# Where the first feed-forward gets its transposed input: in its own blocks, or from layer 0's attention by way of memory

## The chip, the core and the metric

The kernel runs on one core of a Trainium2 chip, in one launch. The metric is the device time of the launch in microseconds (us). A core has five engines that run side by side, each through its own queue of instructions: TensorE (PE in the profile: matrix products and transposes), VectorE (DVE), ScalarE (ACT), GpSimd (POOL) and SyncE (SP, which here only issues transfers). Transfers between the memory outside and the on-chip memory run on 16 DMA engines; SP's queue and POOL's queue both issue them.

## The reference, cut to what matters

Two gated blocks over x, 4 x 1024 rows of 512 numbers. In each, the row is normalised, attention gives s, a feed-forward gives a gate, and x becomes x + s * silu(gate):

```python
x = L0_attn_x
xn = _layernorm(x, axis=-1)                       # eps 1e-5
s = _L0_attn_ref(xn, Wqkv, bqkv, Wout, bout, slopes)
g = _silu(_L0_ffn_ref(xn, w_fc, w_proj))
x = x + s * g
# ... the same again with layer 1's attention and feed-forward

def bitlinear(x, w):                              # in _L0_ffn_ref, twice
    xn = layer_norm(x)                            # eps 1e-6
    ...
    return jnp.einsum('bsd,od->bso', x_hat, w_hat)
```

Layer 0's attention is linear attention with decay, in chunks with a running state. Its input and the feed-forward's input are the same rows: the first bitlinear normalises the already normalised row once more. Doing that a second time only multiplies the row by one number per row (per token), 1 / sqrt(variance of the normalised row + 1e-6).

## The kernel before, in words

The 4096 rows are cut into 8 blocks of 512 (`BLK`), a block into 4 tiles of 128 rows (`TPB`). A block's transposed rows are held as four slabs of 128 features x 512 tokens (`KD`). The program has four stages, one after the other: attention of layer 0, the feed-forward of layer 0, attention of layer 1, the feed-forward of layer 1. The change touches the first two.

**Attention of layer 0** (L234 to L544) is a loop of 32 steps (L506): block `blk`, head group `g` from 0 to 3. A step's products on TensorE are, in this order: `scores` of this step; `project`, which makes queries and keys of the next step from `xnTs[blk]`; a first job (`output` of the block before for g < 2, `values` of the block after for g >= 2); `outs`; the transposes of keys (`turn_k`); for g < 2 two tiles of the next block's rows normalised and transposed (`turn0`); the second job; the product for the state (`states`). Around them, ScalarE adds the bias to kT and qT (L355) and copies `oT` (L451); VectorE weighs the scores into `pt` (L422), makes `kd` (L374), adds the bias to values (L328) and to outputs (L338), and keeps the state; GpSimd makes `qd` (L357). Beside that, two jobs a step from `weights0` load a 256 KB piece of the feed-forward's weights each (`raw0`, two buffers) and reduce it or turn it into its ternary form on VectorE.

`moments0` takes mean and variance of the next block's rows in step g = 0; `norms0` (L302) makes the second normalisation's factor from them and multiplies it with the first one's (L308), so that `st[:, :, 3]` is one factor for both. The normalised rows `xn` have a tag of two buffers; the slabs `xnT` have two as well, so block `blk + 2` overwrites block `blk`; the tag `s` for outputs has two. The single-bank accumulators in PSUM (`acc`) also rotate over two: an accumulator can be started when the one two before it has been read out.

**The feed-forward's input.** Its products take the input as two parts, `hi` (the number rounded to the matmul's format, fp32r) and `lo` (the rest), each 128 x 4 x 512, from `xpair` (tags xp0 and xp1, two buffers each). In attention all four of these buffers hold `wqkv` and a few constants (L255). For block 0 the parts are made in the last step by `first_rows` (L453): x is loaded again (L542), VectorE makes `xq` with the one factor, TensorE transposes it, and `split_in` (L227) copies hi on ScalarE and subtracts lo on VectorE. For the other blocks this is done in the feed-forward itself.

**The feed-forward of layer 0** (L552 to L743) runs over 8 blocks x 16 hidden chunks c. `hidden` multiplies the chunk (8 matmuls, L594), ScalarE applies gelu, casts and squares, VectorE subtracts the low part `hp` (L607), and the sums of h and of its square are kept on GpSimd (L615) and VectorE (L616). `proj` (L647, 8 matmuls a chunk) follows two to eight chunks behind. In blocks 0 to 6, x of the next block is loaded at c = 0, 3, 6 and 9 (L714), `prep_in` makes xq at c = 2, 5, 8 and 11 (L574), and one chunk later `turn_in` transposes it on TensorE (L582) and splits it. `gate` of the block before (L652) comes at c = 1, 3, 5 and 7; it loads x and s. In block 0, six weight pieces are still loaded and made ternary (L718).

**Order.** TensorE's order is written by hand: within `manual_schedule` it runs its instructions as the program lists them. The order on the other queues, SP's included, is chosen when the kernel is built, by when each operation is expected to be ready, and is fixed from then on: an instruction that waits holds up all behind it. `keep_in_program_order` pins an instruction behind the one that the program lists just before it on the same queue; it doesn't hold back later ones that are not pinned. The pools with `reuse_waits="tile"` make the first writer of a buffer wait only for the readers of the tile that had it before.

Of the kernel before, what the change touches and what calls it, by code (L numbers as in the profile page):

```python
# [35 lines left out]
def kernel(ctx, tc, ins, out):  # L36
# [59 lines left out]
    nc.vector.memset(one_i, 1)  # L96

    xnT_d = [dram.tile([KD, P, N], F32, tag=f"xnT{b}", name=f"xnT_d{b}") for b in range(B)]

    def moments(pool, src, dst, name, pinned=False):  # L100

# [122 lines left out]
            w = nxt  # L224
            yield

    def split_in(xp, i, tp):  # L227

        hi, lo = [a[:, :, i * P : (i + 1) * P] for a in xp]
        nc.scalar.copy(hi.bitcast(F32R), tp)  # L230
        nc.vector.tensor_tensor(lo.bitcast(F32R), tp, hi, ALU.subtract)


    with ExitStack() as es:  # L234
# [52 lines left out]


        xnTs, vs, oTs = {}, {}, {}
        xparts = {}  # L290

        def moments0(blk):
            st = st0[blk]
            for i in range(TPB):
# [7 lines left out]
        def norms0(blk):  # L302

            st = st0[blk]
            nc.vector.tensor_tensor(st[:, :, 3], st[:, :, 1], st[:, :, 1], ALU.mult)
            nc.vector.tensor_tensor(st[:, :, 3], st[:, :, 3], st[:, :, 2], ALU.mult)
            inv_std(st[:, :, 3], eps6)
            nc.vector.tensor_tensor(st[:, :, 3], st[:, :, 3], st[:, :, 1], ALU.mult)  # L308

        def turn0(blk, i):  # L310
            st = st0[blk]
# [138 lines left out]
            oTs[blk, g] = p2.tile([P, BLK], F32, tag="oT", name=f"oT0_{nm}", bufs=6)  # L450
            nc.scalar.copy(oTs[blk, g], o)  # L451

        def first_rows(i0):  # L453

            st = st0[0]
            for i in range(i0, i0 + 2):
                xq = p2.tile([P, D], F32, tag="xn", name=f"xq_{i}")
                nc.vector.tensor_scalar(
                    xq, xt.pop(i), st[:, i, 0:1], st[:, i, 3:4], ALU.subtract, ALU.mult
                )  # L460
                tp = tr(f"tr_xq_{i}")
                for k in range(KD):
                    nc.tensor.transpose(tp[:, k, :], xq[:, k * P : (k + 1) * P], ident)
                split_in(xparts[0], i, tp)

        es.enter_context(tc.manual_schedule(engines={mybir.EngineType.PE}))

        st = st0[0]
# [37 lines left out]
        for n, (blk, g) in enumerate(steps):  # L506

            if g < 2:
                jobs = [(output, blk - 1, 2 * g + c) for c in range(2)] if blk else []
            else:  # L510
                jobs = [(values, blk + 1, 2 * g - 4 + c) for c in range(2)] if blk + 1 < NBLK else []
            if n + 1 == len(steps):
                xparts[0] = xpair("xp_0")
                jobs = [(first_rows, 0), (first_rows, 2)]
            if g == 0 and blk + 1 < NBLK:
                moments0(blk + 1)
            pts = scores(blk, g, *cur[:2])
# [34 lines left out]
    with ExitStack() as es:  # L552
# [5 lines left out]
        def tr0(name):  # L558
            return pp.tile([P, KD, P], F32, tag="tr", name=name)

        hparts, sums, mvs, x1s, xnTp, x0fs = {}, {}, {}, {}, {}, {}
# [4 lines left out]
        def prep_in(blk, i):  # L566

            st = st0[blk]
            if i == 0:
                xparts[blk] = xpair(f"xp_{blk}")  # L570
            t = blk * TPB + i
            x = x0fs.pop(t)
            xq = p2.tile([P, D], F32, tag="xq", name=f"xq_{t}")
            nc.vector.tensor_scalar(  # L574
                xq, x, st[:, i, 0:1], st[:, i, 3:4], ALU.subtract, ALU.mult
            )
            return lambda: turn_in(blk, i, xq)

        def turn_in(blk, i, xq):
            tp = tr0(f"tr_xq_{blk}_{i}")  # L580
            for k in range(KD):
                nc.tensor.transpose(tp[:, k, :], xq[:, k * P : (k + 1) * P], ident)  # L582
            split_in(xparts[blk], i, tp)

        before = None

# [65 lines left out]
        def gate(blk, i):  # L652

            t = blk * TPB + i
            mv = mvs[blk]

            last = blk == NBLK - 1 and i >= 2
            x = p2.tile([P, D], F32, tag="x" if last else "xr", name=f"x0r_{t}")
            nc.sync.dma_start(out=x, in_=x_t[t])
            s = p2.tile([P, D], F32, tag="xq" if last else "s", name=f"s0_{t}")  # L660
# [12 lines left out]
            queue.dma_start(out=x1_t[t], in_=th)  # L673
            moments(p2, th, st1[:, t, :], f"c{t}")
# [19 lines left out]
                )  # L694

        es.enter_context(tc.manual_schedule(engines={mybir.EngineType.PE}))
        pending = None
        W = {}
        for g in range(NH0 * NBLK + 2 + 2 * TPB):
            blk, c = divmod(g, NH0)  # L700
            if g == NH0 * NBLK:

                for n in ("wk", "wq", "wv"):
                    W[n] = shared_tile(n, n)
                    tc.keep_in_program_order(
                        nc.gpsimd.dma_start(
                            out=W[n], in_=ins[n + "T"].rearrange("(k p) n -> p k n", p=P)
                        )
                    )
            if blk < NBLK:  # L710
                if c % 3 == 0 and c < 3 * TPB and blk + 1 < NBLK:
                    t = (blk + 1) * TPB + c // 3
                    x0fs[t] = p2.tile([P, D], F32, tag="x", name=f"x0f_{t}")
                    nc.sync.dma_start(out=x0fs[t], in_=x_t[t])  # L714
                if c >= 2 and c % 3 == 2 and c < 2 + 3 * TPB and blk + 1 < NBLK:
                    pending = prep_in(blk + 1, (c - 2) // 3)
                hidden(blk, c)
                if blk == 0 and wpj0 + c < NH0:  # L718
                    ternary("pj", wpj0 + c, raw0("pj", wpj0 + c, "f"))
            for i in range(TPB):  # L720
                q = g - 2 - 2 * i
                if 0 <= q < NH0 * NBLK:
                    proj(q // NH0, i, q % NH0)
            if c == 0 and blk == 1:
                rps = tr0("rows_ps").rearrange("p k c -> p (k c)")
                for w in range(NH0):
                    nc.tensor.matmul(
                        rps, lhsT=onesr, rhs=wpj[w], start=(w == 0), stop=(w == NH0 - 1)
                    )
                nc.scalar.copy(rows, rps)  # L730
            if blk and c == 1:
                stats(blk - 1)
            if blk and c % 2 and c < 2 * TPB:
                gate(blk - 1, c // 2)
            if blk and c == 12:
                norm1(blk - 1, p2)
            if pending and c % 3 == 0:
                pending()
                pending = None
# [764 lines left out]
```

## Time and profile before

| what | value |
|---|---|
| median of 3 runs | 3135.22 us (3134.12 to 3144.06) |
| the profiled execution | 3134.57 us, its span 3132.7 us, mean granted TensorE clock 0.996 |
| attention of layer 0 | 0 to about 605 us, then its last outputs to 620 us |
| feed-forward of layer 0 | 620 to about 1154 us |
| HBM traffic | 104.10 MB read, 41.94 MB written, 47 GB/s over the span |

A row of the profile's groups names a line of the kernel, the engine, the operation, output <- input by the program's names with buffer numbers left out, the shapes, how often it ran, and min/median/max in nanoseconds or busy microseconds and the mean. A row of the timeline begins with start and length in us; in brackets at its end stands the idle time of that engine before it, and what ended it. A row of busy times by stretch gives the stretch and its length, then for each engine its busy us and the number of its records, then the granted clock (1.00 is full speed), the DMA engines' busy share and GB/s. PE is TensorE's matmuls, PEld its weight loads, SPq and POOLq the issue of transfers. Matmuls are pipelined, so the sum of their lengths is more than the time they take.

### The profile page before, as it was taken

The numbers are of one execution on the slowest core, as the hardware profiler recorded it, in microseconds if no ns is written. First come the engines' busy times: TensorE is split into PE (matmuls) and PEld (weight loads), VectorE is DVE, ScalarE is ACT, GpSimd is POOL, SyncE is SP. The second block draws the span as 40 slices with busy tenths as digits, with TensorE's granted clock in tenths as the row PEclk, the third lists the DMA queues.
The fourth block names the chain that finished last, engine by engine and source line by source line (L and its number), as shares of the span: only waits on it lengthen the run. The fifth ranks groups of instructions, "written<-read, shape, count | busy, mean of one in ns | idle before, by whom it ended". The sixth has DMA issues, their size and how long they took to land.

```text
span 3132.7 us, 61075 instructions
## 1 busy us (share of the span) xinstructions
PE 3074.4 (98%) x26241; PEld 1757.1 (56%) x26241; DVE 1878.7 (60%) x2620; ACT 1195.2 (38%) x1696; POOL 1476.2 (47%) x614
## 2 busy tenths in 40 slices
PE   9999999999999997999999999999999999999998
PEld 5555555577777873443344443334444435888887
DVE  4444555478887775556655555555555674566655
ACT  3111111155556542444444444444444444333332
POOL 0000000034443443898888988888888850000001
PEclk9999999999999998999999999999999999999999
DMA  3111111112222331100001000010000013322211
GB/s 132 55 54 61 54 55 41 58 55 87 85 75 68 108 126 39 47 8 8 7 17 41 12 12 15 17 38 13 10 17 12 12 48 112 108 78 64 68 51 55
DMA packets 97543, 158.46 MB, mean 51 GB/s; under 512 B 13040, under 2 KB 26864, under 8 KB 97136
## 3 DMA queue, kind: packets, MB, share of 16 engines
q1 hardware_dynamic: 96128, 150.28, 15.5%
q8 instruction: 207, 3.39, 0.5%
q0 software_dynamic: 1136, 4.19, 0.4%
q14 instruction: 72, 0.59, 0.1%
HBM read 104.10 MB, written 41.94 MB: 47 GB/s over the span
## 4 chain that ended last, share of the span: by engine, by line
PE 58%; DVE 1%; ACT 1%; issue 0%; SPq 0%; DMA 0%; ACTq 0%; DVEq 0%
PE sk L1033 9%; PE sq L1006 8%; PE y L1052 8%; PE gate L1236 5%; PE up L1236 5%; PE dn L1258 5%; PE wq L862 4%; PE v1ps L862 3%; PE wo L862 3%; PE wk L862 3%; PE sk L1039 2%; PE z L946 1%; ACT pT L1044 1%; DVE mT L1022 1%; PE tr_m L1016 1%; DVE mx L1010 0%
## 5 line engine op out<-in xcount | busy, mean ns | idle before, releaser
L1010 DVE TENSOR_REDUCE mx<-sq 128x2 f32<-128x1024 f32 x512 | 603.4, 1218 | 392.5 <-PE sq L1006 391.2
L1075 POOL TENSOR_TENSOR part<-part,pT 128x2048 f32<-128x2048 f32 x180 | 826.7, 4593 | 19.6 <-ACT pT L1044 10.8
L1044 ACT ACTIVATE pT<-sk 128x1024 f32<-128x1024 f32 x512 | 496.2, 1021 | 611.9 <-PE sk L1039 606.8
L1006 PE MATMUL sq<-wkT,wqT 32*128 32x512 f32 x2048 | 321.3, 640 | 13.3 <-POOL wqT L920 7.2
L1033 PE MATMUL sk<-wqT,wkT 32*128 32x512 f32 x2048 | 326.0, 639 | 4.1 <-DVE mx L1010 3.8
L1052 PE MATMUL y<-pT,v 128*32 128x512 f32 x2048 | 273.7, 605 | 0.1
L615 POOL TENSOR_TENSOR sums<-sums,h 128x512 f32<-128x512 f32 x112 | 164.0, 1465 | 227.6 <-ACT h L599 222.4
L647 PE MATMUL pj<-wpj,hp 128*128 128x512 f32 x1024 | 265.2, 397 | 5.8 <-DVE hp L607 4.8
L594 PE MATMUL fc<-xp,wfc 128*128 128x512 f32 x1024 | 260.8, 397 | 2.9 <-ACT h L599 2.0
L1280 POOL TENSOR_TENSOR th<-th,x 128x512 f32<-128x512 f32 x31 | 40.1, 1295 | 457.6 <-DVE th L1279 378.9
L1039 PE MATMUL sk<-mT,onesr 2*128 2x512 f32 x1024 | 236.6, 785 | 0.0
L350 PE MATMUL qk<-xnT,wqkv 128*128 128x512 f32 x512 | 228.3, 599 | 0.7 <-ACT xnT L148 0.7
L357 POOL TENSOR_TENSOR qd<-qT,wqkv 128x512 f32<-128x512 f32 x32 | 40.7, 1272 | 397.3 <-ACT qT L355 372.2
L647 PEld LDWEIGHTS pj<-wpj,hp 128*128 128x128 f32 x1024 | 189.9, 188 | 58.0 <-DVE hp L607 17.4
L594 PEld LDWEIGHTS fc<-xp,wfc 128*128 128x128 f32 x1024 | 187.3, 188 | 44.3 <-ACT h L599 5.1
L1236 PE MATMUL gate<-xp,wf 128*128 128x512 f32 x704 | 174.1, 389 | 0.0
L1236 PE MATMUL up<-xp,wf 128*128 128x512 f32 x704 | 173.9, 389 | 0.0
L1258 PE MATMUL dn<-wf,hp 128*128 128x512 f32 x704 | 173.6, 389 | 0.0
L1033 PEld LDWEIGHTS sk<-wqT,wkT 32*128 32x128 f32 x2048 | 98.0, 183 | 133.5 <-issue 109.8
L1073 POOL TENSOR_TENSOR part<-pT,pT 128x2048 f32<-128x2048 f32 x30 | 136.7, 4558 | 67.6 <-ACT pT L1044 67.4
L607 DVE TENSOR_TENSOR hp<-h,hp 128x512 fp32r<-128x512 f32 x128 | 117.1, 915 | 76.2 <-ACT hp L604 76.2
L1006 PEld LDWEIGHTS sq<-wkT,wqT 32*128 32x128 f32 x2048 | 89.5, 183 | 125.9 <-issue 83.4
(229 smaller groups left out, 4512.4 us busy)
## 6 DMA issues: line engine op xcount, KB each, us to landing
s<-s SPq DMA_DIRECT2D x96, 256.0 KB
x<-x SPq DMA_DIRECT2D x36, 256.0 KB
x<-in_x SPq DMA_DIRECT2D x32, 256.0 KB
raw_fc<-in_w_fcT SPq DMA_DIRECT2D x32, 256.0 KB
x0f<-in_x SPq DMA_DIRECT2D x32, 256.0 KB
x0r<-in_x SPq DMA_DIRECT2D x32, 256.0 KB
xnT<-xnT_d SPq DMA_DIRECT2D x8, 1024.0 KB
s<-so SPq DMA_DIRECT2D x32, 256.0 KB
```

What stands on the lines that cost most here:

```text
L594: nc.tensor.matmul(a, lhsT=wfc[k][:, c * P : (c + 1) * P], rhs=xp[n][:, k, :].bitcast(F32R), start=(k == 0 and n == 0), stop=(k == KD - 1 ...
L647: nc.tensor.matmul(ds[i], lhsT=hparts[blk, c][n][:, i * P : (i + 1) * P], rhs=wpj[c], start=(c == 0 and n == 0), stop=(c == NH0 - 1 and n ...
L862: nc.tensor.matmul(out[r0 : r0 + HD, :], lhsT=lhsT[:, r0 : r0 + HD], rhs=rhs, start=start, stop=stop,)
L1006: nc.tensor.matmul(sq[:, hh, :], lhsT=qT[r, q0 : q0 + P], rhs=kT[r, n * 512 : (n + 1) * 512], start=True, stop=True,)
L1010: nc.vector.tensor_reduce(mx[:, qt, 2 * pair : 2 * pair + 2, n], sq, AX.X, ALU.max)
L1033: nc.tensor.matmul(sks[h // 2][:, h % 2, :], lhsT=kT[r, kb * P : (kb + 1) * P], rhs=qT[r, qh * 512 : (qh + 1) * 512], start=True, stop=False,)
L1039: nc.tensor.matmul(sks[h // 2][:, h % 2, :], lhsT=onesr[r, :], rhs=mTs[u][r, :], start=False, stop=True,)
L1044: nc.scalar.activation(pT[:, 2 * pair : 2 * pair + 2, :], sks[pair], AF.Exp, scale=QKS)
L1052: nc.tensor.matmul(y[r, :], lhsT=v[:, kb, r], rhs=pT[:, h, :], start=(kb == 0), stop=(kb == TB - 1),)
L1075: add.tensor_tensor(parts[u], parts[u], pT, ALU.add)
L1236: nc.tensor.matmul(a, lhsT=ws[n, c][:, k, :], rhs=xp[m][:, k, :], start=(k == 0 and m == 0), stop=(k == KD - 1 and m == 1),)
L1258: nc.tensor.matmul(ds[i], lhsT=hparts[blk, c][n][:, i * P : (i + 1) * P], rhs=w, start=(c == 0 and n == 0), stop=(c == NH1 - 1 and n == 1),)
```

## The change

The 1e-6 factor is no longer multiplied into the 1e-5 one; its 512 numbers for a block are stored in memory by POOL's queue. At the end of step g = 2 of each block, `scale` loads them back as one row on all partitions and GpSimd multiplies the block's four slabs with it in place: after that step no product of attention reads the slabs any more. In step g = 3, before `outs`, `split` makes hi on ScalarE (in the two buffers of the tag xn) and lo on VectorE (in place), slab by slab, and POOL's queue stores both in memory: eight transfers of 256 KB a block, 16.8 MB in all. `ffn_in` loads a block's two parts, 1 MB each, on SP's queue: for block 0 at the end of the last step but one of attention, for the others at c = 1 of the block before. `first_rows`, `prep_in`, `turn_in`, `split_in`, their reloads of x and their 128 transposes are gone.

```diff
+    xp0_d = [
+        [dram.tile([KD, P, BLK], F32, tag=f"xp0_{i}_{m}", name=f"xp0_d{i}_{m}") for m in range(2)]
+        for i in range(NBLK)
+    ]
+    more_d = dram.tile([NBLK, BLK], F32, tag="more", name="more_d")
...
-    def split_in(xp, i, tp):
-
-        hi, lo = [a[:, :, i * P : (i + 1) * P] for a in xp]
-        nc.scalar.copy(hi.bitcast(F32R), tp)
-        nc.vector.tensor_tensor(lo.bitcast(F32R), tp, hi, ALU.subtract)
+    def ffn_in(blk):
+
+        xparts[blk] = xpair(f"xp_{blk}")
+        for m in range(2):
+            tc.keep_in_program_order(
+                nc.sync.dma_start(out=xparts[blk][m], in_=xp0_d[blk][m].rearrange("k p n -> p k n"))
+            )
...
             inv_std(st[:, :, 3], eps6)
-            nc.vector.tensor_tensor(st[:, :, 3], st[:, :, 3], st[:, :, 1], ALU.mult)
+            nc.gpsimd.dma_start(out=more_d[blk].rearrange("(i p) -> p i", p=P), in_=st[:, :, 3])
+
+        def scale(blk):
+
+            more = mores[blk] = p2.tile([P, BLK], F32, tag="s", name=f"more_{blk}")
+            tc.keep_in_program_order(
+                nc.sync.dma_start(out=more, in_=more_d[blk].partition_broadcast(P))
+            )
+            for k in range(KD):
+                x = xnTs[blk][:, k, :]
+                tc.keep_in_program_order(nc.gpsimd.tensor_tensor(x, x, more, ALU.mult))
+
+        def split(blk, k):
+
+            x = xnTs[blk][:, k, :]
+            hi = p2.tile([P, BLK], F32, tag="xn", name=f"hi_{blk}_{k}")
+            tc.keep_in_program_order(nc.scalar.copy(hi.bitcast(F32R), x))
+            tc.keep_in_program_order(
+                nc.vector.tensor_tensor(x.bitcast(F32R), x, hi, ALU.subtract)
+            )
+            for m, part in enumerate((hi, x)):
+                tc.keep_in_program_order(nc.gpsimd.dma_start(out=xp0_d[blk][m][k], in_=part))
...
-            if n + 1 == len(steps):
-                xparts[0] = xpair("xp_0")
-                jobs = [(first_rows, 0), (first_rows, 2)]
...
             if jobs:
                 jobs[0][0](*jobs[0][1:])
+            if g == 3:
+                for k in range(KD):
+                    split(blk, k)
             outs(blk, g, cur[2], pts)
...
             cur = nxt
+            if g == 2:
+                scale(blk)
             if n + 2 == len(steps):
-
-                for i in range(TPB):
-                    xt[i] = p2.tile([P, D], F32, tag="x", name=f"x0f_{i}", bufs=4)
-                    tc.keep_in_program_order(nc.sync.dma_start(out=xt[i], in_=x_t[i]))
+                ffn_in(0)
...
-                if c % 3 == 0 and c < 3 * TPB and blk + 1 < NBLK:
-                    t = (blk + 1) * TPB + c // 3
-                    x0fs[t] = p2.tile([P, D], F32, tag="x", name=f"x0f_{t}")
-                    nc.sync.dma_start(out=x0fs[t], in_=x_t[t])
-                if c >= 2 and c % 3 == 2 and c < 2 + 3 * TPB and blk + 1 < NBLK:
-                    pending = prep_in(blk + 1, (c - 2) // 3)
+                if c == 1 and blk + 1 < NBLK:
+                    ffn_in(blk + 1)
...
-            if pending and c % 3 == 0:
-                pending()
-                pending = None
```

The last block's gate, which borrowed the buffers of x and xq for two tiles, gets tags of its own for them (`xl`, `sl`).

More of the change, by code (lines that the diff above doesn't have):

```diff
@@ L225, in weights0 @@
             yield
-    def split_in(xp, i, tp):
-        hi, lo = [a[:, :, i * P : (i + 1) * P] for a in xp]
-        nc.scalar.copy(hi.bitcast(F32R), tp)
-        nc.vector.tensor_tensor(lo.bitcast(F32R), tp, hi, ALU.subtract)
+    xparts = {}
+    def ffn_in(blk):
[4 more added lines that the diff above has]
+            )
     with ExitStack() as es:
@@ L289 @@
         xnTs, vs, oTs = {}, {}, {}
-        xparts = {}
+        mores = {}
         def moments0(blk):
@@ L451, in outs @@
             nc.scalar.copy(oTs[blk, g], o)
[L453 to L464, printed above, removed]
         es.enter_context(tc.manual_schedule(engines={mybir.EngineType.PE}))
@@ L559, in tr0 @@
             return pp.tile([P, KD, P], F32, tag="tr", name=name)
-        hparts, sums, mvs, x1s, xnTp, x0fs = {}, {}, {}, {}, {}, {}
+        hparts, sums, mvs, x1s, xnTp = {}, {}, {}, {}, {}
         for c in range(wpj0, NH0):
@@ L564 @@
         rows = p2.tile([P, D], F32, tag="rows", name="rows", bufs=1)
[L566 to L583, printed above, removed]
         before = None
@@ L657, in gate @@
             last = blk == NBLK - 1 and i >= 2
-            x = p2.tile([P, D], F32, tag="x" if last else "xr", name=f"x0r_{t}")
+            x = p2.tile([P, D], F32, tag="xl" if last else "xr", name=f"x0r_{t}")
             nc.sync.dma_start(out=x, in_=x_t[t])
-            s = p2.tile([P, D], F32, tag="xq" if last else "s", name=f"s0_{t}")
+            s = p2.tile([P, D], F32, tag="sl" if last else "s", name=f"s0_{t}")
             nc.sync.dma_start(out=s, in_=s0_t[t])
@@ L736 @@
                 norm1(blk - 1, p2)
-            if pending and c % 3 == 0:
-                pending()
-                pending = None
             if 0 < blk < NBLK and c >= 14:
```

## The prediction

> **What bounds the kernel now.** I read the first page, then a table of busy time by stage, then the timeline of one attention step and of the feed-forward's last two blocks. The page says that TensorE sets the time:
>
> ```profile
> span 3132.7 us, 61075 instructions
> PE 3074.4 (98%) x26241; PEld 1757.1 (56%) x26241; DVE 1878.7 (60%) x2620; ACT 1195.2 (38%) x1696; POOL 1476.2 (47%) x614
> ```
>
> So whatever leaves TensorE's queue shortens the span by what it held there, and added work costs only where TensorE comes to wait for it. Next, the busy time by stage (columns: stretch, PE, PEld, DVE, ACT, POOL, granted clock, DMA share, GB/s): attention of layer 0, the turn into the feed-forward with its first block, and the feed-forward's seven other blocks.
>
> ```profile
> 30.00:605.00 575.00, 567.83 (x3685) 317.62 (x3684) 282.51 (x574) 83.06 (x139) 44.10 (x47) 1.00 0.16 52
> 605.00:684.00 79.00, 74.60 (x305) 54.69 (x304) 47.08 (x61) 35.47 (x58) 21.25 (x15) 1.00 0.24 74
> 684.00:1147.00 463.00, 456.83 (x2118) 367.60 (x2117) 373.80 (x626) 265.28 (x441) 203.35 (x140) 1.00 0.26 82
> ```
>
> In attention VectorE is half idle, ScalarE and GpSimd almost wholly, the DMA engines too. In the feed-forward VectorE is 81% busy. The change carries work from the second kind of stage to the first. The tile of what is removed:
>
> ```profile
> L582 PE MATMUL tr_xq<-ident,xq x112: 270/272/301, 629.8 to 1065.9; 128*128 128x128 f32 x112
> L574 DVE TENSOR_SCALAR xq<-x0f,st x28: 509/534/1608, 623.4 to 1050.1; 128x512 f32<-128x512 f32 x28
> L463 PE MATMUL tr_xq<-ident,xq x16: 272/273/328, 599.8 to 605.6; 128*128 128x128 f32 x16
> ```
>
> 272 ns is not the price, since matmuls overlap. The price can be read from two blocks: block 6 makes block 7's input, block 7 makes none. From each block's c = 2 to the same matmul group of c = 13:
>
> ```profile
> 1021.24:1067.81 46.57, 45.73 (x206) 36.33 (x206) 42.33 (x69) 24.92 (x42) 23.02 (x15) 1.00 0.35 111
> 1087.42:1131.83 44.41, 43.68 (x191) 34.82 (x191) 38.33 (x61) 22.97 (x38) 22.85 (x15) 1.00 0.29 95
> ```
>
> The 15 or 16 more PE records in the first are the four transposed tiles; it is 2.16 us longer, 0.54 us a tile.
>
> **Part by part, removed.**
> - *Feed-forward blocks 1 to 6:* 6 x 2.16 = 13.0 us off TensorE's queue. The transposes alone are 0.46 a tile there (0.36 to the next matmul, and that group takes 1.93 instead of 1.84), the rest is a wait for VectorE near c = 8 that block 7 does not have. Waits for ScalarE and VectorE at c = 9 and 10 stand in block 7 as well (0.43 and 0.25), so I expect them to stay.
> - *Block 0:* four tiles x 0.46 = 1.8, and one 1.9 us wait of a transpose for xq (642.50). Three waits of pj for hp (0.65, 0.67, 0.32) may shrink too, VectorE being full from 630 to 650; I count nothing for them.
> - *Attention's last step (L453 to L464):* oT's matmuls end at 604.1 and output begins at 605.74, after 0.7 of waiting and eight transposes. The first eight (599.84) only fill the wait for pt. So 1.6; bounds 0.9 (the second eight alone, if another wait takes the gap) and 2.5 (both groups and the wait).
>
> Sum removed: 13.0 + 1.8 + 1.9 + 1.6 = 18.3 us. VectorE also loses 28 x (0.53 + 0.68) and ScalarE 28 x 0.57 us, which are off the path beyond the waits named.
>
> **Added in attention, once a block.** I lay it on block 3. Its step g = 2 starts with its scores at 286.73, g = 3 at 304.81.
> - *more_d's store* (512 single floats, POOL's queue) replaces the small product L308. Its load comes two steps (36 us) later in block 0 and six steps later in the others. Behind it on POOL stand qd, used one step later, and the state copy. No row has such small pieces; from nothing to a few us of POOL's idle 7 to 17 us. I take 0.
> - *scale:* the load of 256 KB goes behind this step's raw loads on SP (issued to 292.6), and lands near 296.5 if it takes the 3.9 us below. SP has nothing urgent behind it. Then four GpSimd products like qd (128x512, 1267 ns): 297.1 to 302.2, before split at 313.84. xnT's last readers, the (3,3) projections, end at 295. Cost 0, with 11 us of cover.
> - *split:* four ScalarE copies (0.59 each, as oT), four VectorE subtractions (0.68, as L607), eight stores of 256 KB from POOL's queue. The step, and who is late if they block:
>
> ```profile
> 313.15 0.69 ACT L355 ACTIVATE qT<-qk,bqk 128x512 f32<-128x512 f32 x1 [2.75 <-PE qk L350]
> 313.92 1.27 POOL L357 TENSOR_TENSOR qd<-qT,wqkv 128x512 f32<-128x512 f32 x1 [16.82 <-ACT qT L355]
> 316.52 0.69 DVE L328 TENSOR_TENSOR v<-v0ps,wqkv 128x512 f32<-128x512 f32 x1 [6.23 <-PE v0ps L324]
> 318.45 0.58 ACT L451 COPY oT<-o 128x512 f32<-128x512 f32 x1 [4.62 <-PE o L445]
> 319.01 0.69 DVE L374 TENSOR_TENSOR kd<-k0t,kdec 128x512 f32<-128x512 f32 x1 [1.80 <-PE k0t L372]
> 322.25 1.44 PE L388 MATMUL u<-v,kd 128*128 128x128 f32 x8
> 322.45 0.69 DVE L328 TENSOR_TENSOR v<-v0ps,wqkv 128x512 f32<-128x512 f32 x1 [2.74 <-PE v0ps L324]
> ```
>
> hi has two buffers (tag xn), so hi_2 waits for hi_0's store to land. The only stores from POOL's queue here:
>
> ```profile
> L673 POOL DMA_DIRECT2D x<-th x4: 542/551/560, 1156.7 to 1164.6; - x4
> DMA to landing us min/median/max: 2.6/3.9/4.4
> ```
>
> Worked out: hi_0 and hi_1 by 315.0; hi_0's store is issued when qd ends, 315.2, and lands at 319.1; lo_0 waits for v's addition and ends at 317.9; then two issues of 0.55, so hi_1's store starts at 318.45 and lands at 322.4. hi_2 is ready at 319.7, hi_3 at 323.0, lo_3 at 323.7. TensorE looks next for kd and oT's freed bank at 322.25 (kd ended 319.70, oT 319.03: 2.6 and 3.2 us of cover), and for v's bank at 325.18 (323.14: 2.0). If ScalarE and VectorE take oT, kd and v as they come, nothing is late: 0. If lo_3 stands ahead of kd, kd ends at 324.4 and TensorE loses 2.1 us a block. A gain is excluded, since split takes nothing off TensorE. I take 0.25, nearer the free end because the later oT, kd and v are not pinned behind the waiting ones: 8 x 0.25 = 2 us. If POOL waits for lo_3, the state copy behind it comes at about 325 as now (325.64).
> - *Buffers:* block 3's xnT is overwritten for block 5 from about 338, and its last store lands near 328; xn's buffer is wanted at 332. Both are clear.
>
> *The skill against the rows.* The Trainium skill (SBUF — State Buffer, "Who interferes with whom") says that a VectorE instruction with two SBUF inputs and a GpSimd one that reads SBUF shut each other out for a whole instruction, and ("SBUF: two separate sides") that stores issued from GpSimd starve while VectorE runs in a two-port mode, 0.62 us becoming 3.1. It speaks against scaling on GpSimd and storing from it. The first holds here: L308 takes 169 ns, and 1236 under a qd. But between 297 and 302 VectorE has only v and kd, which read PSUM, and L328 never passes 692 ns and L374 never 693 beside qd. For the second, hardly anything between 315 and 324 is of the kind it names (subtractions and PSUM reads), and L673's issues took 0.55 among such work. By the rule at each of the three issues before hi_3 the landing is 7 us later and TensorE loses up to 9 us a block; by the row, 2.1 at most. I take the row and keep the rule for the slow rival.
>
> **Added elsewhere.** ffn_in(0) waits on SP for qd(7,3) at 596.9, ahead of output's stores, which come from 609; its 2 MB, at the 236 GB/s that 620 to 630 reached, end near 606, beside 2 MB of split's stores; fc starts at 620.5. Free; 14 us of cover. ffn_in(1) waits for vb and boutb (620.4), and then stands ahead of raw tiles 11 to 15 on SP: 2 MB is 8.9 us, less about 1 MB of x0f loads that are gone. VectorE's ternary of tile 11 ran at 630.3 and could be some us late with hp behind it. From 0 (its slots on VectorE come later anyway) to 6; I take 1. Later blocks' 2 MB have 60 us, and their gates' loads come some 15 us after: 0.
>
> **Sum.** -18.3 + 2 + 1 = -15.3. The profiled execution took 3134.57 (span 3132.7 and 1.9 around it), so 3119.3; it stands 0.65 below the median 3135.22. I say 3119.
>
> **Rivals.**
> 1. *The feed-forward's start is held* by the 2 MB ahead of the raw tiles, 6 to 9 us: 3124 to 3128. For: SP takes its queue in order and VectorE already waited 3.0 us for an x0f here. Against: VectorE is over 3 us freer. 0.13.
> 2. *Split's wait takes the gain's place:* lo_3 ahead of kd in every block, 8 x 2.1 = 17: about 3134. For: the copies are pinned. Against: only behind what came before them. 0.13.
> 3. *Slower:* the same place with slow landings. With L from issue to landing, TensorE's loss is L - 1.8 a block; to pass the gain and 0.3% it must be 3.5, so L above 5.3 us in every block. At L = 6, 34 us: about 3150. For: no row shows eight stores in a row from POOL; against: L673's worst is 4.4 and the DMA engines are 16% busy. 0.12.
> The main case has 0.62, its own range 3112 to 3125.
>
> **The numbers.** A measurement can tell about 0.3% (9.4 us) from no change: faster means below 3125.8. That is the main case and over half of the first rival, 0.70; within it the rest of that and the second, 0.18; slower 0.12. The range runs from 3112 (no new wait; the 1.6 us of block 0's hp waits, the 0.9 more of the last step, and part of the 0.5 a block at c = 9 and 10 gone too) to 3136, over the second rival.
>
> **What would show it.** No tr_xq; blocks 1 to 6 of the feed-forward at about 64.4 instead of 66.6 us; output starting right after oT; attention's g = 3 steps still 18 to 19 us. Wrong if u waits for kd or oT in those steps (rivals 2, 3), or if neg_pj waits for raw_pj_f near 630 (rival 1).

## The result, and the profile after

The changed kernel takes 3125.84 us (median of 6 runs, 3123.44 to 3130.27). The kernel before, run beside it, takes 3141.31 (6 runs, 3134.12 to 3148.05). The ratio is 0.9956, 95% interval 0.9941 to 0.9971, so 9 to 19 us are gone. A second set of 6 runs gives 3124.53 against 3140.56, ratio 0.9950 (0.9934 to 0.9967). Both differences of medians, 15.5 and 16.0 us, are near the 15.3 of the prediction's sum. But the sum was made against a profiled run of 3134.57, at the low end of what the kernel before shows, and the profiled run of the changed kernel takes 3125.21: 9.4 us less. Profile against profile, 6 us of the forecast are missing. Where they went is the main question here.

The first page of the changed kernel; 128 matmul records are gone, VectorE is 19 us less busy, GpSimd 78 us more:

```profile
span 3123.4 us, 61054 instructions
PE 3065.9 (98%) x26113; PEld 1746.9 (56%) x26113; DVE 1860.0 (60%) x2580; ACT 1198.6 (38%) x1696; POOL 1554.1 (50%) x718
```

Busy time by stage, columns as before: attention of layer 0, the turn with the first block, the seven other blocks.

```profile
30.00:608.00 578.00, 569.49 (x3664) 317.43 (x3666) 297.61 (x591) 101.55 (x178) 122.45 (x144) 1.00 0.28 84
608.00:684.00 76.00, 73.38 (x309) 53.26 (x302) 44.38 (x52) 34.36 (x56) 24.51 (x22) 1.00 0.39 135
684.00:1131.00 447.00, 442.02 (x2014) 357.90 (x2012) 341.48 (x580) 254.62 (x417) 200.25 (x140) 1.00 0.29 94
```

GpSimd went from 44 to 122 us in attention, the DMA engines from 16 to 28%; VectorE from 81 to 76% of the seven blocks. Block 6 from c = 2 to c = 13, which took 46.57, is now like block 7 before (44.41):

```profile
1008.20:1052.57 44.37, 43.66 (x190) 34.82 (x190) 38.33 (x61) 22.99 (x38) 22.85 (x15) 1.00 0.30 95
```

The two profiles side by side, by the starts of the same instructions in the timeline of TensorE:

| event | before | after | gap | since the row above |
|---|---|---|---|---|
| scores of step (0,0) | 35.38 | 38.37 | +3.0 | +3.0 |
| scores of (7,3) | 598.73 | 603.43 | +4.7 | +1.7 |
| first feed-forward product | 620.52 | 623.56 | +3.0 | -1.7 |
| last group of it | 1137.70 | 1122.47 | -15.2 | -18.3 |
| first scores of layer 1 | 1182.1 | 1166.4 | -15.7 | -0.5 |
| last scores of layer 1 | 2577.0 | 2567.3 | -9.7 | +6.0 |

The middle of the table is the prediction's sum, and more: +1.7 for the split, -1.7 for the last step, -18.3 for the feed-forward. The two losses that it did not count are 3.0 us before the first scores and 6.0 us in a stage that the change doesn't touch.

The only new wait in attention that TensorE shows is the split's, in block 5 (timeline; in brackets the idle time before and what ended it):

```profile
477.34 0.62 ACT L333 CAST hi<-xnT 128x512 fp32r<-128x512 f32 x1 [3.46 <-DMA xp_d<-hi]
477.99 0.69 DVE L335 TENSOR_TENSOR xnT<-xnT,hi 128x512 fp32r<-128x512 f32 x1 [3.31 <-ACT hi L333]
478.60 0.68 DVE L358 TENSOR_TENSOR v<-v0ps,wqkv 128x512 f32<-128x512 f32 x1
479.34 0.49 PE L418 MATMUL u<-v,kd 128*128 128x128 f32 x2 [1.42 <-DVE v L358]
```

Read upwards it is a chain: the store of hi_1 lands, hi_3 may be written, lo_3 can be made, v's last tile comes behind it on VectorE, and the last two matmuls of u wait 1.42 us. The stores behave as the row of L673 said, except for the longest:

```profile
L338 POOL DMA_DIRECT2D xp_d<-xnT x32: 540/542/555, 95.4 to 615.2; - x32
DMA to landing us min/median/max: 2.3/2.7/6.8
```

### The profile page after: what moved, and what is told of

Same layout as the page of the kernel before. It is cut to its first block, busy times and chain, and to the rows that moved or that the text cites. A ratio compares the mean times of both kernels' runs of the same rounds, so it can differ in the third digit from the quotient of the medians.

```text
span 3123.4 us, 61054 instructions
## 1 busy us (share of the span) xinstructions
PE 3065.9 (98%) x26113; PEld 1746.9 (56%) x26113; DVE 1860.0 (60%) x2580; ACT 1198.6 (38%) x1696; POOL 1554.1 (50%) x718
## 3 DMA queue, kind: packets, MB, share of 16 engines
q1 hardware_dynamic: 101120, 160.77, 17.1%
## 4 chain that ended last, share of the span: by engine, by line
PE 58%; DVE 2%; ACT 1%; issue 0%; SPq 0%; DMA 0%; ACTq 0%; DVEq 0%
PE sk L1022 9%; PE sq L995 8%; PE y L1041 8%; PE gate L1225 5%; PE up L1225 5%; PE dn L1247 5%; PE wq L851 4%; PE v1ps L851 4%; PE wo L851 3%; PE wk L851 3%; PE sk L1028 2%; PE z L935 1%; DVE mT L1011 1%; ACT pT L1033 1%; PE tr_m L1005 1%; DVE mx L999 0%
## 5 line engine op out<-in xcount | busy, mean ns | idle before, releaser
L604 DVE TENSOR_TENSOR hp<-h,hp 128x512 fp32r<-128x512 f32 x128 | 129.2, 1009 | 85.8 <-ACT hp L601 85.4
L380 PEld LDWEIGHTS qk<-xnT,wqkv 128*128 128x128 f32 x512 | 95.6, 192 | 113.5 <-issue 106.4
```

Of the source, the lines that this page charges most:

```text
L380: nc.tensor.matmul(a, lhsT=wqkv[k][:, c0 : c0 + P], rhs=xnTs[blk][:, k, :], start=(k == 0), stop=(k == KD - 1),)
```

## The experiments

Theory at the start: the gain of the feed-forward is the transposes' place in TensorE's queue, the split costs 1.7 us by the chain just shown, and the two other losses are chance of TensorE's clock. The rivals: the feed-forward's gain is the relief of VectorE and ScalarE; the opening is slow because of more_d's store. Times below are medians beside the kernel before in the same set of runs; "steps" are the starts of the 32 scores against those of before, counted from the first.

**The changed kernel again**, unedited.

> The changed kernel once more, for the two stretches in which its first profile lost time that no wait explains: the opening (first scores at 38.4 instead of 35.4 us) and a dip of the granted clock near 2520 us in attention of layer 1 (6 us). Theory A, both are chance of TensorE's clock: this profile has its own values, at least one of the two being absent or elsewhere; attention of layer 0 from the first scores on, and the feed-forward of layer 0, repeat within 0.5 us. Theory B, the change causes the slow opening (the 512 four-byte pieces of more_d hold the DMA engines while constants are loaded): the first scores stand at 38.4 again.

Measured: 3124.53, as above. The theory of chance did not hold as stated: both losses are there again. The first scores stand at 37.81 and the next step 0.93 later still; and near 2520 us the clock drops again, as in the first profile. First the clock, changed kernel, then its repeat (columns as in the stage table):

```profile
2500.00:2520.00 20.00, 18.81 (x138) 6.33 (x136) 16.90 (x13) 8.37 (x10) 14.42 (x4) 0.99 0.18 54
2520.00:2540.00 20.00, 19.37 (x90) 6.04 (x90) 13.76 (x13) 6.83 (x9) 13.27 (x4) 0.67 0.14 40
```

```profile
2520.00:2540.00 20.00, 19.62 (x90) 6.15 (x90) 13.75 (x13) 6.87 (x8) 13.28 (x4) 0.66 0.14 40
```

A granted clock of 0.67 over 20 us is 6.6 us of work lost. That it is near the 6.0 of the table is in part chance: from one group of scores to the next against those of before, 5.5 us are lost at the clock's drop, 1.9 us near 2220 us at full clock, and about 1.3 us come back elsewhere in the stage. The 1.9 us are a wait for VectorE, whose instruction for mT falls beside a GpSimd product. The changed kernel, then the same place before:

```profile
2216.97 4.55 POOL L1064 TENSOR_TENSOR part<-part,pT 128x2048 f32<-128x2048 f32 x1
2217.08 4.99 DVE L1011 SCALAR_TENSOR_TENSOR mT<-mh,second,mf 128x512 fp32r<-128x512 f32 x1 [0.50 <-ACT mh L1009]
2223.26 0.70 PE L1022 MATMUL sk<-wqT,wkT 32*128 32x512 f32 x2 [0.76 <-DVE mx L999]
```

```profile
2230.64 4.55 POOL L1075 TENSOR_TENSOR part<-part,pT 128x2048 f32<-128x2048 f32 x1
2234.00 1.75 DVE L1022 SCALAR_TENSOR_TENSOR mT<-mh,second,mf 128x512 fp32r<-128x512 f32 x1 [0.50 <-ACT mh L1020]
```

mT ends about 0.55 us after `part` in both; it takes 0.74 us at best. Over 4 us it takes five times in each profile of before and six times in each of the changed kernel, so this too goes with where the two engines happen to meet. The slice ahead of the clock's drop has its TensorE idle for 1.2 us in all. The first profile of the kernel before has the same gaps at the same work (the longest 0.73 us) and keeps a clock of 1.00 there, and so does its repeat.

Then the opening. In the first profile TensorE's clock is at half speed from 10.9 to 17.7 us, a loss of 3.4, and u waits no longer than before (0.95 us); its 3.0 us are the clock. In the repeat the clock is whole until the wait, so another cause can be read:

```profile
26.37 4.79 ACT L508 ACTIVATE dec<-cst,slb 128x128 f32<-128x128 f32 x16 [3.63 <-DMA cst<-in_c_decay]
31.18 2.29 DVE L509 TENSOR_TENSOR dec<-dec,cst 128x2048 f32<-128x2048 f32 x1 [3.97 <-ACT dec L508]
35.35 0.68 DVE L404 TENSOR_TENSOR kd<-k0t,kdec 128x512 f32<-128x512 f32 x1
36.09 1.79 PE L418 MATMUL u<-v,kd 128*128 128x128 f32 x8 [2.30 <-DVE kd L404]
```

The constant cst lands at 26.4 (before: 21.2), so dec is 5 us late, v's last tiles and kd queue behind it on VectorE, and u waits 2.30 instead of 0.94 us. After that TensorE's clock is at half speed for part of 36 to 40 us. And cst is late while the DMA engines, from 16 to 24 us, move little although they are busy. The kernel before, then the changed one:

```profile
16.00:24.00 8.00, 8.00 (x20) 3.61 (x19) 0.69 (x1) 5.62 (x15) 0.00 (x0) 1.00 0.97 333
```

```profile
16.00:24.00 8.00, 8.00 (x18) 3.52 (x17) 0.05 (x1) 3.17 (x5) 0.00 (x0) 0.89 0.79 65
```

Busy share 0.79 with 65 GB/s, where it was 0.97 with 333. What was added there is the store of 512 numbers of 4 bytes, issued at 11.81; the eight stores of this kind take 9.3 to 12.8 us to land (8.5 to 11.0 in the repeat). The Trainium skill (DMA: Bandwidth & Descriptors, "Specifications") asks for 512 bytes a piece for the full rate and says that smaller ones are read and written back; the rows agree in kind, and show others beside it slowed: cst lands about 5 us later. That the store is the cause is tested below.

**The kernel before again**, one run.

> The kernel before once more. Theory A (the clock by chance): the first scores stand at 35.4 or later, and the dips of layer 1 fall elsewhere, so that the stages before 1160 us repeat within 0.5 us while the last two differ by several. Theory B (the change makes the opening slow): 35.4 again.

Measured: 3133.86, first scores at 35.58, all steps, the feed-forward (517.0) and even the stretches of half clock as in the first profile. (1 - clock) times length, without the half-clock stretch that ends every profile, is 8.5 us lost in both profiles of before, 17.1 in both of the changed kernel. So in these four profiles the clock's losses go with the kernel; two profiles of each don't show that they always do.

**The added part alone.** The kernel before, which also stores, scales and splits as the change does; what it stores is not read.

```diff
+            nc.vector.tensor_copy(st[:, :, 4], st[:, :, 3])
+            nc.gpsimd.dma_start(out=more_d[blk].rearrange("(i p) -> p i", p=P), in_=st[:, :, 4])
...
+            if g == 3:
+                for k in range(KD):
+                    split(blk, k)
...
+            if g == 2:
+                scale(blk)
```

> The added part alone: the kernel before, which also stores the factor, scales, splits and stores in attention; nobody reads what it stores, and the feed-forward makes its own input as before. The theory from the two profiles: the split costs 1.7 us over 8 blocks, by u's wait for v behind lo_3, and the first feed-forward is unchanged, so the time is 2 us over the kernel before (up to 5 with a slow opening). Rival 2 of the prediction: 17 us. If the transfers or the GpSimd work cost something hidden in the comparison of the two profiles, between these.

Measured: 3153.84 against 3140.56, ratio 1.0044 (1.0028 to 1.0060). In the steps the theory holds: 0.25, 0.21 and 1.06 us at the same three places, 1.5 in all, and first scores at 38.29. The feed-forward is unchanged (516.9). But 9.9 us more are lost from the last scores to the feed-forward, which this mixture makes itself: xq and hi share the tag xn there, and xq waits behind hi for stores to land. 8.0 of them come ahead of the output's products, 1.9 in these, with the clock at half speed for 10.2 us from 611.7.

```profile
614.88 0.55 DVE L488 TENSOR_SCALAR xq<-x0f,st 128x512 f32<-128x512 f32 x1 [0.34 <-DMA xp_d<-hi]
615.57 1.09 PE L493 MATMUL tr_xq<-ident,xq 128*128 128x128 f32 x4 [6.67 <-DVE xq L488]
```

So the total says nothing of the change, the steps do.

**The transposes back, alone:**

```diff
+            if blk + 1 < NBLK and c in (3, 6, 9, 12):
+                tp = tr0(f"idle_{blk}_{c}")
+                for k in range(KD):
+                    nc.tensor.transpose(tp[:, k, :], ident, ident)
```

> The changed kernel with four transposes of a constant back in the feed-forward's c = 3, 6, 9 and 12 of blocks 0 to 6, for every tile; nobody reads them, and VectorE and ScalarE get no work back. Theory: the 18.4 us that the feed-forward became shorter are mostly the transposes' place in TensorE's queue: 28 x 0.46 = 12.9 us are given back, the feed-forward takes about 516 us instead of 503, and the remaining 5.5 are VectorE's and ScalarE's relief. Rival: TensorE waits for h, hp and the sums in a block anyway, and the gain is the relief of VectorE (28 x 1.2 us) and ScalarE; the transposes then fill waits and give back under 5 us.

Measured: 3134.53 against 3140.56, ratio 0.9978 (0.9965 to 0.9991), 10 us over the changed kernel. The feed-forward (first to last group) takes 508.0 us, where the changed kernel's two profiles have 498.9 and 498.6: some 9.2 of the 18.3 us. Neither expectation was right. By the distances between the fc groups of blocks 2 to 6, the four tiles cost 0.46, 0.40, 0.16 and 0.44 us. The third, at c = 9, falls into a wait that is there anyway. The changed kernel:

```profile
975.10 2.11 PE L591 MATMUL fc<-xp,wfc 128*128 128x512 f32 x8 [0.43 <-ACT h L596]
977.69 1.90 PE L644 MATMUL pj<-wpj,hp 128*128 128x512 f32 x7 [0.25 <-DVE hp L604]
```

with transposes alone:

```profile
982.53 0.60 PE L732 MATMUL idle<-ident 128*128 128x128 f32 x4
983.14 2.13 PE L591 MATMUL fc<-xp,wfc 128*128 128x512 f32 x8
```

and before:

```profile
986.40 0.60 PE L582 MATMUL tr_xq<-ident,xq 128*128 128x128 f32 x4
987.26 2.09 PE L594 MATMUL fc<-xp,wfc 128*128 128x512 f32 x8 [0.26 <-ACT h L599]
```

The transposes alone fill the 0.43 us; in the kernel before, the wait for h comes on top of them.

**The other engines' half back, alone:** VectorE's product and subtraction and ScalarE's cast for 28 tiles, in SBUF, not read by anyone.

```diff
+                    nc.vector.tensor_scalar(
+                        xq, xparts[blk][0][:, i, :], st0[blk][:, i, 0:1], st0[blk][:, i, 3:4],
+                        ALU.subtract, ALU.mult,
+                    )
...
+                nc.scalar.copy(xh.bitcast(F32R), pending)
+                nc.vector.tensor_tensor(pending.bitcast(F32R), pending, xh, ALU.subtract)
```

> The changed kernel with the other half of the removed work back in the feed-forward, without transposes: for 28 tiles VectorE's product (in SBUF), ScalarE's cast and VectorE's subtraction at c = 2 to 12, on data that nobody reads. With the transposes alone back, the feed-forward took 9.2 of the 18.3 us back. Theory: the two halves add up, this one gives back the other 9 us by waits of pj and fc for hp and h (feed-forward about 508 us). Rival: with the transposes gone TensorE and the others have room for it, and it costs under 3; then the 9 us need both together.

Measured: 3127.15 against 3136.54, ratio 0.9969 (0.9959 to 0.9979); the feed-forward takes 501.5, 2.6 to 2.9 us more than the two profiles of the changed kernel, nearly all of it in block 0. The rival holds: in blocks 1 to 6 this half is nearly free (0.1 us in all).

**Both halves as a chain:** as the last, but the product is transposed on TensorE and the cast and the subtraction read the transposes. The reloads of x are missing.

```diff
+                tp = tr0(f"tr_xq_{blk}_{c}")
+                for k in range(KD):
+                    nc.tensor.transpose(tp[:, k, :], pending[:, k * P : (k + 1) * P], ident)
...
+                nc.scalar.copy(xh3.bitcast(F32R), tp)
+                nc.vector.tensor_tensor(xl3.bitcast(F32R), tp, xh3, ALU.subtract)
```

> The changed kernel with both halves of the removed work back in the feed-forward as one chain, as it stood before: VectorE's product, four transposes of it, ScalarE's cast and VectorE's subtraction out of PSUM, for 28 tiles, on data that nobody reads; only the reloads of x are missing. Transposes alone gave 9.2 us back, the other engines' half alone 2.9. Theory: the remaining 6 come from the chain, an engine that waits for another one's half in the middle of a block, and the feed-forward takes 516 to 517 us as before the change. Rival: they come from something else, such as the loads of x, and it takes 498.6 + 12 = 511.

Measured: 3146.12 against 3138.32, ratio 1.0020 (1.0009 to 1.0032). The feed-forward takes 519.5, with a half-clock stretch of 1.7 us in block 0 that the others lack; so about 517.8, all of the gain and a little more. In the sum the theory holds: 9.2 is the transposes' own place, up to 2.9 the other engines', and the remaining 6 to 7 come back only with both as a chain, without the reloads of x. Most are where c = 9 is: 1.0 us a block there in blocks 3 to 6, against 0.16 with transposes alone. The places agree only in part: the kernel before also loses 0.4 us at c = 12 in blocks 1 to 5 (0.75 to 0.81 us over the changed kernel there, this run 0.35), and this run loses 0.25 at c = 14 in these blocks, which the kernel before doesn't. So for some 2 us the chain is argued, not shown. How the chain lengthens that wait (VectorE's late subtraction ahead of the gate's products, they ahead of ScalarE's tanh, and that ahead of h) was read from the order of the rows; no run took one link of it away.

**Block 0's factor stored later**, after step 0 instead of in the opening:

```diff
-            nc.gpsimd.dma_start(out=more_d[blk].rearrange("(i p) -> p i", p=P), in_=st[:, :, 3])
+            if blk:
+                keep_more(blk)
...
+            if n == 0:
+                keep_more(0)
```

> The changed kernel with block 0's store of the factor (512 pieces of 4 bytes) moved from the opening to the end of step 0. Four profiles so far, two of each sort, put the first scores at 35.4 and 35.6 without this store and at 38.4 and 37.8 (plus 0.9 to the next step) with it. Theory: the pieces hold the DMA engines while cst and kj load, dec comes 5 us late, v and kd behind it on VectorE, and TensorE waits or finds its clock halved. Then the first scores stand at 35.2 to 35.6 and the next step follows after 12.77 us, so all that follows comes 3 to 3.7 us earlier, the span is about 3120 to 3121. Rival, the clock's chance alone: some 38 us again, or a value between.

Measured: 3121.86 against 3136.54, ratio 0.9949 (0.9934 to 0.9963). First scores at 37.20, which looks like the rival. The rows divide it:

```profile
21.86 4.78 ACT L517 ACTIVATE dec<-cst,slb 128x128 f32<-128x128 f32 x16
36.11 1.16 PE L427 MATMUL u<-v,kd 128*128 128x128 f32 x8 [0.94 <-DVE kd L413]
```

dec starts at 21.9 without waiting for cst, and u waits the 0.94 of before: what the store did is gone. What is left is the clock, at half speed for part of 12 to 18 us: the first 16 projections took 8.83 us instead of 7.13, just the 1.7 by which 37.20 exceeds 35.5. So the store and the clock were both at work, and each shows in a row of its own; the clock drops in the opening without the store too. In the medians the store's cost doesn't show: 0.9949 of the kernel before, where the changed kernel has 0.9956 and 0.9950. In the nine profiles with the early store, dec starts at 25.5 to 27.6; in the four without, at 21.2 to 23.3.

**Four buffers for hi:**

```diff
-            hi = p2.tile([P, BLK], F32, tag="xn", name=f"hi_{blk}_{k}")
+            hi = p2.tile([P, BLK], F32, tag="xn" if k < 2 else "s", name=f"hi_{blk}_{k}")
```

> The changed kernel with four buffers for hi in a block instead of two (slabs 0 and 1 in the tag xn, slabs 2 and 3 in the tag s, which is free at that time), so that no copy waits for a store to land. Theory: the 1.7 us that attention loses from step to step (0.2, 0.2 and 1.3 us behind blocks 1, 3 and 5) come from hi_2 and hi_3 waiting for landings, with lo_3 ahead of v's last tile on VectorE; all three vanish, and the time falls by 1.7 us, too little for the clock's scatter to show but plain in the profile's steps. Rival: they come from the traffic itself or from GpSimd's work, and stay.

Measured: 3120.40 against 3136.54, ratio 0.9942 (0.9927 to 0.9957). All 32 steps stand within 0.01 us of those before. Block 5 again:

```profile
466.15 2.16 ACT L333 CAST hi<-xnT 128x512 fp32r<-128x512 f32 x4
474.66 1.44 PE L418 MATMUL u<-v,kd 128*128 128x128 f32 x8
474.86 0.69 DVE L358 TENSOR_TENSOR v<-v0ps,wqkv 128x512 f32<-128x512 f32 x1 [2.23 <-PE v0ps L354]
```

Four copies in one piece, and v's last tile waits for TensorE, not TensorE for it. The theory holds; the traffic and GpSimd's products cost the steps nothing.

**Slabs 2 and 3 split later**, two buffers as in the change, one run:

```diff
             if jobs:
                 jobs[1][0](*jobs[1][1:])
+            if g == 3:
+                for k in range(2, KD):
+                    split(blk, k)
```

> The changed kernel with slabs 2 and 3 split after the second job of the step instead of ahead of outs; two buffers for hi as in the change. Theory (order): what costs is only that lo_3 stands ahead of v's last tile on VectorE when the next block is one whose u reads that tile; with lo_3 behind it the waits for landings remain, and the steps lose 0.0 instead of 0.2, 0.2 and 1.3. Rival (waits): the copies that wait for landings hold oT or kd instead, and the steps lose as much or more.

Measured: 3127.36, steps within 0.02 us of before. So the order on VectorE suffices: with lo_3 behind v, TensorE doesn't meet the wait for a landing. (Its first scores stand at 38.30, with the store in the opening and 1.7 us of half clock.)

**Every part stored twice:**

```diff
                 tc.keep_in_program_order(nc.gpsimd.dma_start(out=xp0_d[blk][m][k], in_=part))
+                tc.keep_in_program_order(nc.gpsimd.dma_start(out=twice_d[blk][m][k], in_=part))
```

> The changed kernel with each part stored a second time into another tensor that nobody reads, so that hi's buffers come free later and twice the traffic leaves in g = 3. The prediction's slow rival says that TensorE's loss grows one for one with the time to landing. Theory: it holds; two more issues of 0.55 us and a landing some 1 to 3 us later put lo_3 and v behind it 2 to 4 us later in each block, and attention loses 12 to 30 us over 8 blocks instead of 1.7. Rival: the landings overlap, the queue has room, and attention loses under 5.

Measured: 3122.70 against 3136.54, ratio 0.9948 (0.9929 to 0.9968). The prediction's slow rival fell: after the opening, attention loses 0.98 us in all, in one place (the first step of block 3), and nothing behind blocks 1, 3 and 5. The landing's median did rise, from 2.7 to 3.9 us, and a copy waits 3.98 us for the second store:

```profile
478.29 0.69 DVE L363 TENSOR_TENSOR v<-v0ps,wqkv 128x512 f32<-128x512 f32 x1 [2.05 <-PE v0ps L359]
479.38 0.62 ACT L337 CAST hi<-xnT 128x512 fp32r<-128x512 f32 x1 [3.98 <-DMA tw_d<-hi]
480.03 0.69 DVE L339 TENSOR_TENSOR xnT<-xnT,hi 128x512 fp32r<-128x512 f32 x1 [1.05 <-ACT hi L337]
```

But lo_3 now stands behind v on VectorE, as in the run with the later split. VectorE's order is chosen when the kernel is built; here lo_3 was put later. So the loss became smaller although the landings took longer; but since the order changed with them, the run doesn't tell what a slow landing costs in the order of the changed kernel.

**Three mends together:** four buffers, block 0's factor after step 0, and two products without readers after each transpose of the opening to keep TensorE's clock up.

```diff
+        def still(n):
+            for _ in range(n):
+                nc.tensor.matmul(warm[:, :P], lhsT=ones, rhs=ones, start=True, stop=True)
...
                 turn0(0, i - 1)
+                still(2)
```

> The changed kernel with three mends together: four buffers for hi, block 0's store of the factor after step 0, and two idle products after each of the opening's transposes, so that TensorE isn't idle while it waits for rows (their results are not read). Theory: no stall is left in attention (steps as before, +0.0), first scores at 35.3 to 35.8, the feed-forward stays at 498.6 us, so that TensorE's work alone puts it 20 us under the kernel before; what the clock does in layer 1 (1.7 us for each window at half speed, 6.8 to 12 us lost in the profiles so far) decides the rest: median 3114 to 3120. Rival: the opening's clock still drops, and it is level with the kernel that has four buffers alone (3120).

Measured: 3119.60 against 3138.32 (6 runs, 3117.85 to 3122.79), ratio 0.9936 (0.9921 to 0.9951): the lowest median of the study, level with four buffers alone (3120.40), whose profile happened to lose only 1.0 us in the opening. First scores at 35.68, steps within 0.01, feed-forward 498.3; its last group is at 1117.8, 4.7 us ahead of the changed kernel and 19.9 ahead of before. Near 2520 us its clock is 1.00, but 1.7 us each are lost in two other places of layer 1. The idle products were not run alone, so what they do for the clock is not shown.

## Why the prediction was right, and where not

The direction, its cause and the size of the sum held. That the medians' difference meets the sum within 1 us is in part luck: more was gained in the feed-forward and less lost at ffn_in(1) than forecast, the opening and layer 1 lost what no step had, and the runs of the kernel before have a median 6 to 7 us above the profiled run that the sum was made against. By the prediction's own steps:

- *Feed-forward, 13.0 + 3.7 - 1 = 15.7 expected, 18.3 measured.* Blocks 3 and 5 became 2.6 us shorter, 66.6 to 64.0, block 6 only the 2.18 of the twins. The twin was not typical: block 6 of before lacks 0.4 us at c = 12 that blocks 1 to 5 have (4.03 against 4.45 us from one fc group to the next). Blocks 1 to 6 together gave 14.9 instead of 13.0. The working's split of the 2.16 into transposes at 0.46 each and a wait near c = 8 that block 7 lacks was right in kind: by the runs 1.5 of 2.6 us is the transposes' own place. The waits at c = 9 and 10 stayed, as said (0.43 and 0.25).
- *Block 0 (3.7) and ffn_in(1) (1 us lost).* Block 0 gave 3.4. The wait for xq is gone, the waits of pj for hp stayed (0.73, 0.77, 0.34), and the raw tiles came in time: the 1 us counted for ffn_in(1) was not lost. Rival 1 did not happen.
- *Attention's last step, 1.6:* from the scores of (7,3) to the first output product 7.01 became 5.34, so 1.67.
- *split, 2.0 expected, 1.7 measured,* but not a quarter of a microsecond in each block. The working named kd, oT's bank and v's bank; the deadline that bound was v's last tile itself, which u's last matmuls read, 2 us before the bank is wanted. It bites only in blocks 1, 3 and 5: their next block's u takes four chunks, that of an odd block three. Rivals 2 and 3 named kd, and were wrong in place and price; the formula of L - 1.8 a block, made for lo_3 ahead of kd, met no run with that order and stays untested.
- *scale and ffn_in(0), 0:* right, no step shows them.
- *more_d's store, 0 expected: this step failed.* The working looked at what queues behind it on GpSimd, in the middle of attention. The cost is in block 0, on the DMA engines, in the one stretch where these are full (333 GB/s). To the second step's scores the nine profiles that have it there are 1.0 to 4.2 us behind before, 0 to 3.4 of it as half clock, which the run with the later store has as well (1.7). What the store alone cost is the wait: u waited 1.4 us longer in the repeat.
- *Not in the sum at all: TensorE's clock in layer 1.* In the profiled run 6.0 us are given back there, 5.5 at the clock's drop and 1.9 at VectorE's wait beside GpSimd, less some small gains. The change adds nothing in that stage. Two profiles of it drop near 2520 us and two of before don't; of eight edited forms of it three lose as much there, two half as much, three nothing. What decides the drop stays open. The losses in the opening and in layer 1 are what the forecast of 3119 lacked against 3125.8, at the edge of the main case's 3112 to 3125. The difference of medians met the sum nevertheless, since the profile of before that the sum was made against was a fast one: it had lost 8.5 us to the clock, and most other executions of that kernel took longer at a lower mean clock.

## What to carry to other kernels

When work moves from a full stage to an idle one, cost it where the resource it uses is full, which may be the first of its repeats: here one transfer of 2 KB in the opening made TensorE wait 1.4 us in the repeat, nearly as much as eight times eight stores of 256 KB in mid-stage (1.7). For an added wait, list everything behind it on the same queue and, for each, the earliest reader, not only the buffer's next writer; then ask whether the order or the buffer is cheaper to change (one more pair of free buffers took the whole 1.7 us away, and so did the later split). And take a sum's base from several runs: with a TensorE that is 98% busy, a few short stretches at half clock are as large as the change.

## What the runs showed of the hardware

- Small pieces hold DMA engines out of proportion: 512 pieces of 4 bytes took 9.3 to 12.8 us to land; in the opening the engines' busy share was then 0.79 for 65 GB/s, and a constant on another queue landed about 5 us later, which it did not when the store was moved.
- The granted clock fell to 0.50 in the middle of steady work. The largest idle gap ahead of the stretch at 2520 us is 0.72 us. The stretches at half clock in these profiles, but for the one at the end, lasted 3.4, 6.8, 10.2 or 13.7 us, so 1.7, 3.4, 5.1 or 6.8 us were lost in each. The Trainium skill (TensorE: Matmul & The Clock Gate, "Part 1: The HAM clock gate") says half clock follows an idle window of 3.4 us; its note on a "second HAM failure mode", many short gaps, fits these rows better. No run here shows which gaps decide.
- Stores of 256 KB from GpSimd's queue kept 0.54 us an issue and a median landing of 2.7 us beside VectorE's subtractions, 3.9 with twice as many. The starving that the prediction weighed did not appear.
- VectorE's mT (128x512) took 0.74 us at best and up to 5.0 us beside a GpSimd product of 4.55 us; it ended about 0.55 us after that one.
